# Two Mamba layers on one core: constants cast by ScalarE, projection weights in two tiles loaded in pieces, and a reordered last image

## The chip, the cores and the metric

The kernel runs on one core of one Trainium2 chip. The metric is the device time of one execution in microseconds (us). Three runs are shown for the kernel before, and one further execution was recorded by the hardware profiler.

## The reference, cut to what matters

The input is x, 8 images of 384 channels and 32 x 32 pixels in float32. Four residual layers follow, each on a group norm (32 groups) of x.

```python
x = x + L0(_gn(x))   # Mamba over the 1024 pixels of an image
x = x + L1(_gn(x))   # 1x1 conv, 8x8 FFT filter, depthwise 3x3, gelu(x1)*x2, 1x1 conv
x = x + L2(_gn(x))   # layer norm, Mamba, then gelu(t @ w1.T + b1) @ w2.T + b2
x = x + L3(_gn(x))   # depthwise 3x3 convolution

# Mamba, d_inner 768, 16 states
xin, z = split(xseq @ in_proj_w.T)
u = silu(causal_conv3(xin) + conv_b)
dt, B, C = split(u @ x_proj_w.T);  dt = softplus(dt @ dt_proj_w.T + dt_proj_b)
h = exp(dt*A) * h + (dt*u) * B     # step by step over the pixels
y = (sum_n(h * C) + u*D) * silu(z)
return y @ out_proj_w.T
```

## The kernel before, in words

The pixels of an image make two chunks of T = 512, so each Mamba layer has 16 chunks and both together have 32, numbered n = 0 to 31. Chunks 0 to 15 are layer 0, followed image by image by layer 1 (`layer1`); chunks 16 to 31 are layer 2 with its MLP (`mlp`), followed image by image by layer 3 (`layer3`). A chunk has NQ = 24 scan steps, 768 in all. One step reads 1 MB of dt*u from DRAM into a tile `g` of 128 partitions x 4 x 512 (`begins`, on the SP queue), multiplies it by B on GpSimd (`times`), makes dt by a matmul into the four banks `dA` (`decays`), takes the exponential on ScalarE (`exps`), scans on VectorE (`scans`), multiplies by C half on GpSimd (`states`) and half on VectorE, and sums the states by matmuls into `y` (`gathers`). After four steps a block of 128 channels of y is gated by silu(z) (`gatings`); six blocks make a chunk. Five `g` tiles are in rotation, so the load of step t waits for the sums of step t - 5.

`front(n)` prepares a chunk: norm, the input projection `ps_in` into u, silu, `ps_x`, `ps_dt`, and the DMAs dtd and dud that hand dt and dt*u over through DRAM. `gates(n, h)` makes one half of silu(z) by the projection `ps_z`. `finish(n)` makes the output projection `ps_out` (3 chains of 6 matmuls), and in layer 2 starts `mlp`: per half g, six chains `ps_up` into the tile `h`, an exact gelu over `h` in two instructions, three chains `ps_dn`.

The text writes no order by hand: every one of these pieces is a Python generator, and `Order.run` picks the next instruction by modelled clocks (`Clocks`), due times, `pace` (not before scan step t) and `once` (a condition). What it picks is a fixed order of instructions for each engine and for the SP queue, which issues all DMAs one after the other; at run time each instruction then waits for its own operands, and everything behind it on its queue waits too.

Places that matter below. At the start VectorE casts the constant `selr` (L400) and scales `minus` (L412) before it takes the statistics of the first image (`measure_first`). `load_mamba` (L508) loads all weights of a Mamba layer; it is called from `front` of chunk 0 and of chunk 16. The tile `w_in` has one buffer and holds both halves of the input projection, for u and for z, so layer 2's weights replace layer 0's:

```python
        w["in"] = new(wk, [P, KC, 2 * DI], F32, "w_in")
        for k in range(KC):
            sync.dma_start(w["in"][:, k, :], a[pre + "in_proj"][k * P : (k + 1) * P, :])
```

In `layer3` an image is normed block by block (k = 0, 1, 2) into one padded tile `xp`; each half of a block gets 4 of its 9 taps as matmuls with a diagonal matrix `diag` (made by ScalarE) into `ps_dw`, and the other 5 by VectorE on the PSUM bank. The next block may be normed only when the last has been taken: `yield once(lambda: taken[0] == 2 * k)`.

In the trace nearly all instructions carry L189, the line of the helper that records them, so groups are told apart by their tiles. A float32 matmul shows as two rows of PE.

Of the kernel before, what the change touches and what calls it, by code (L numbers as in the profile page):

```python
# [48 lines left out]
PATIENCE = 6.0  # L49
TAPS, LAST_TAPS = 4, 4  # L50
SHARE = (2, 2, 2, 2)
# [3 lines left out]
def _flat(ap):  # L55
    return ap.rearrange("p a b -> p (a b)")
# [193 lines left out]
def tile_conv_preact_d4(ctx: ExitStack, tc: tile.TileContext, a: dict, out: bass.AP):  # L250
# [148 lines left out]
    sync.dma_start(sel32, a["c_selr"])  # L399
    vector.tensor_copy(_flat(selr), sel32)  # L400
    selbc = const.tile([RX, 2 * P], F32, name="selbc")
# [3 lines left out]
    eps_gn = const.tile([P, 1], F32, name="eps_gn")  # L405
    vector.memset(eps_gn, GN_EPS)
    eps_ln = const.tile([P, 1], F32, name="eps_ln")
    vector.memset(eps_ln, LN_EPS)
    eye = const.tile([P, P], F32, name="eye")
    sync.dma_start(eye, a["c_eye"])  # L410
    minus = const.tile([P, P], BF16, name="minus")
    vector.tensor_scalar_mul(minus, eye, -1.0)  # L412
    carry = const.tile([P, 4 * NQ], F32, name="carry")
# [6 lines left out]
    ln_mean = const.tile([P, P], F32, name="ln_mean")  # L420
    vector.memset(ln_mean, 1.0 / C)

# [4 lines left out]
    xk_free, m_free, x_free = Tokens(1), Tokens(2), Tokens(3)  # L427
    dt_free, pc_free = Tokens(2), Tokens(2)


# [74 lines left out]
    def load_rows(tile_, src, k=KC):  # L505
        sync.dma_start(tile_, src.rearrange("(k p) l -> p k l", k=k))

    def load_mamba(pre):  # L508
        w = {}
        w["vec"] = new(wk, [P, ND, 5], F32, "w_vec", 2)  # L510
        sync.dma_start(w["vec"], a[pre + "vec"])
        w["A"] = new(wk, [P, 4 * NQ], F32, "w_A", 2)
        sync.dma_start(w["A"], a[pre + "A"])
        w["in"] = new(wk, [P, KC, 2 * DI], F32, "w_in")
        for k in range(KC):
            sync.dma_start(w["in"][:, k, :], a[pre + "in_proj"][k * P : (k + 1) * P, :])
        w["x"] = new(wk, [P, ND, RX], F32, "w_x")
        load_rows(w["x"], a[pre + "x_proj"], ND)
        w["dt"] = new(wk, [RX, DI], F32, "w_dt")
        sync.dma_start(w["dt"], a[pre + "dt_proj"])  # L520
        layer_w[pre] = w
        yield on("ACT", w["A"])
        act(w["A"], w["A"], AF.Exp)
        yield on("DVE", w["A"])
        vector.tensor_scalar_mul(w["A"], w["A"], -1.0)

    def load_out(w, pre):
        w["out"] = new(wk, [P, ND, C], F32, "w_out")
        load_rows(w["out"], a[pre + "out_proj"], ND)

    def projection(s, name, at):
        return chain(
            name, ((s["w"]["in"][:, k, at : at + P], s["xn"][:, k, :]) for k in range(KC))
        )
# [13 lines left out]
    def gates(s, h):  # L548
        n = s["n"]
        yield once(lambda: "normed" in s and (n == 0 or chunks[n - 1]["gated"] >= (NH if h == 0 else ND)))  # L550
        z = s["z", h] = new(wk, [P, NH, T], F32, "z", 2)

        def block(d):
            ps, tag = yield from projection(s, "ps_z", DI + (h * NH + d) * P)
# [39 lines left out]
    def front(s):  # L594
# [5 lines left out]
        else:  # L600
            xn = s["xn"] = new(wk, [P, KC, T], F32, "xf", 2)
            sync.dma_start(xn, _rows(s["src"][s["b"], :, c * T : (c + 1) * T]))
        if n % (B * NCH) == 0:
            yield from load_mamba(s["pre"])
        w = s["w"] = layer_w[s["pre"]]
# [13 lines left out]
        def block(d):  # L619
            if n not in (0, B * NCH - 1, B * NCH):  # L620
                yield pace(s["t"] - 18 + d)
            ps, tag = yield from projection(s, "ps_in", d * P)
# [12 lines left out]
        yield from together(due, [block(d) for d in range(ND)])  # L635
        if c > 0:
            yield on("POOL", *u, due=-1)
# [12 lines left out]
        for h in range(2):  # L650
# [3 lines left out]
            "ps_x", ((w["x"][:, d, :], u[d]) for d in range(ND)), place=lambda ps: ps[:RX, :]  # L654
        )
        yield once(lambda: n == 0 or "fronted" in chunks[n - 1])
        yield on("ACT", ps)
# [251 lines left out]
    def finish(s):  # L909
        n, t = s["n"], s["t"]  # L910
        last = s["pre"] == "l2_"
        due = t + NQ + (10 if not last else 23 if s["c"] == 0 else 16)
        yield once(lambda: s["gated"] == ND and (n == 0 or "free" in chunks[n - 1]))

# [9 lines left out]
        else:  # L924
# [5 lines left out]
            s["tt"] = [new(p2, [P, T], F32, "t", KC) for _ in range(KC)]  # L930

        def block(m):
            ps, tag = yield from chain(
                "ps_out",
# [221 lines left out]
    def mlp(s, due):  # L1156
        x = s["x"]

        def weight(q):
            return lambda: None if q >= len(s["loaded"]) else clocks.known(s["loaded"][q])  # L1160

        for g in range(2):
# [4 lines left out]
            def up(f):  # L1167
# [24 lines left out]
            turn = Tokens(1)  # L1192
# [26 lines left out]
    def layer3(s):  # L1219
# [4 lines left out]
        def blocks():  # L1224
            for h in range(2):
                for k in range(KC):
                    yield h, k, x[h][:, k, :], None

        gn = yield from group_stats(blocks)
        taken = [0]  # L1230
        taps = TAPS if b < B - 1 else LAST_TAPS
        for k in range(KC):
            yield once(lambda: taken[0] == 2 * k)
            for h in range(2):
                yield on("ACT", gn[1])
                group_norm(
                    xp[:, 1 + 16 * h : 17 + 16 * h, 1 : W + 1], _img(x[h][:, k, :]), gn
                )
            for hf in range(2):
                yield pace(s["t"] + NQ + 20 + (7 if b < B - 2 else 4) * (2 * k + hf))  # L1240
                rows = slice(hf * 512, (hf + 1) * 512)

                def window(dy, dx, hf=hf):
                    return xp[:, 16 * hf + dy : 16 * hf + dy + 16, dx : dx + W]

                def take(ps, tag, k=k, hf=hf, rows=rows, window=window):
# [6 lines left out]
                    yield on("DVE", ps, when=lambda: 0.0 if taken[0] == 2 * k + hf else None)  # L1253
                    acc = new(p2, [P, T], F32, "acc")
                    vector.tensor_add(acc, ps, x[hf][:, k, :])
# [44 lines left out]
    def diagonal():  # L1300
        yield once(lambda: len(chunks[0].get("dtd", ())) > 0)
        yield on("SP")
# [10 lines left out]

    order.add(measure_first(), 0)
    order.add(front(chunks[0]), 0)
    order.add(begun(), 0)
# [152 lines left out]
```

## Time and profile before

| | us |
|---|---|
| runs: median (lowest to highest of 3) | 6279.72 (6264.88 to 6286.1) |
| profiled execution: own time | 6281.34 |
| profiled execution: span of the trace | 6279.6 |
| busy: PE | 5835.6 (93%) |
| busy: GpSimd (POOL) | 5720.2 (91%) |
| busy: VectorE (DVE) | 5623.6 (90%) |
| busy: ScalarE (ACT) | 4234.9 (67%) |

Times within the trace count from the start of the span. A row of the timeline has the start, the time taken (of all instructions merged into it), the engine, the tiles and the count; the bracket at its end gives the idle time before it on that engine and what ended it. "SPq" rows are issues of DMAs, and a merged row's time runs from its first issue to its last. "PEclk" is the granted clock of TensorE as a share of full speed. Mean granted clock over the execution was 0.965.

### The profile page before, as it was taken

The page shows a single profiled execution, that of the slowest core. Times are in us where ns is not written, and L with a number is a line of the kernel's source. Part 1 is how long each engine was busy: PE and PEld are TensorE (multiplying, and loading weights), DVE is VectorE, ACT ScalarE, POOL GpSimd, SP SyncE. Part 2 cuts the span into 40 slices and gives each one's busy share as a digit, 9 for nine tenths or more (in the row PEclk, how much of TensorE's full clock was granted, in tenths as well). Part 3 has the DMA queues.
Part 4 walks back from the last instruction along what each step waited for, and adds up shares of the span by engine and source line. Part 5 has one row for each costly group of instructions (what it writes and reads, how often), then busy time and mean ns, then how long its engine had stood idle before and what let it go on. Part 6 is the DMA issues. An engine that isn't in the chain of part 4 may idle for free.

```text
span 6279.6 us, 62636 instructions
## 1 busy us (share of the span) xinstructions
PE 5835.6 (93%) x19010; PEld 2196.0 (35%) x19010; DVE 5623.6 (90%) x6392; ACT 4234.9 (67%) x7940; POOL 5720.2 (91%) x2022
## 2 busy tenths in 40 slices
PE   6878999999999999989989999999999999999997
PEld 2223333333333333333333333333333333333333
DVE  4999989999999989988887999999998999989992
ACT  4656677677767667766676766777677676667752
POOL 4999989999998999989997999999999999999980
PEclk8889999999999999999999999999999999999998
DMA  6877878887887878877777888888787787887871
GB/s 174 189 186 185 193 186 194 206 189 192 195 191 182 193 197 199 200 183 179 185 178 182 203 205 208 213 201 209 191 214 195 196 208 189 207 203 197 197 186 35
DMA packets 345860, 1195.88 MB, mean 190 GB/s; under 512 B 40420, under 2 KB 142484, under 8 KB 247220
## 3 DMA queue, kind: packets, MB, share of 16 engines
q1 hardware_dynamic: 345524, 1191.88, 78.0%
q8 instruction: 152, 2.49, 0.2%
q14 instruction: 184, 1.51, 0.1%
HBM read 1040.73 MB, written 150.99 MB: 190 GB/s over the span
## 4 chain that ended last, share of the span: by engine, by line
DVE 18%; PE 14%; POOL 12%; ACT 7%; issue 5%; DMA 3%; SPq 0%; DVEq 0%; POOLq 0%; ACTq 0%
POOL g L189 10%; DVE g L189 8%; DVE dA L189 5%; PE ps_up L189 3%; PE ps_dn L189 2%; PE y L189 2%; DMA g<-dud 2%; DVE ps_dw L189 2%; ACT dA L189 2%; PE dA L189 2%; DVE u L189 1%; PE ps_dw L189 1%; ACT h L189 1%; ACT L370 1%; ACT L189 1%
## 5 line engine op out<-in xcount | busy, mean ns | idle before, releaser
L189 POOL TENSOR_TENSOR g<-g,bc 128x1024 f32<-128x1024 f32 (+1 forms) x1536 | 5241.0, 3445 | 279.4 <-ACT carry L189 111.8
L189 ACT ACTIVATE dA<-dA,w_A 128x512 f32<-128x512 f32 x3072 | 2018.6, 661 | 964.1 <-PE dA L189 952.5
L189 PE MATMUL dA<-dts,selr 96*128 96x512 bf16 x3072 | 1193.7, 391 | 248.1 <-DVE g L189 223.7
L189 DVE TENSOR_TENSOR_SCAN g<-dA,carry,g 128x512 f32<-128x512 f32 x768 | 954.7, 1270 | 70.8 <-POOL g L189 55.2
L189 DVE TENSOR_TENSOR g<-dA,bc 128x512 f32<-128x512 f32 x1536 | 994.5, 678 | 20.4 <-ACT carry L189 18.8
L189 DVE TENSOR_TENSOR_SCAN dA<-dA,carry,g 128x512 f32<-128x512 f32 x768 | 953.8, 1273 | 42.6 <-ACT dA L189 42.1
L189 DVE TENSOR_TENSOR_SCAN dA<-dA,g 128x512 f32<-128x512 f32 x768 | 910.2, 1212 | 65.8 <-ACT dA L189 65.5
L189 DVE TENSOR_TENSOR_SCAN g<-dA,g 128x512 f32<-128x512 f32 x768 | 908.0, 1209 | 61.8 <-POOL g L189 43.9
L189 PE MATMUL y<-g,sely 128*32 128x512 f32 x6144 | 866.9, 632 | 47.0 <-POOL g L189 44.4
L189 PEld LDWEIGHTS <-selr 96*128 96x128 bf16 x3072 | 300.8, 99 | 1117.6 <-issue 1070.2
L189 PE MATMUL ps_in<-xf,w_in 128*128 128x512 f32 x1152 | 574.0, 619 | 3.7 <-ACT xf L189 3.3
L189 PE MATMUL ps_dn<-h,mw 128*128 128x512 f32 x1152 | 556.5, 605 | 13.9 <-ACT h L189 8.0
L189 PE MATMUL ps_z<-xf,w_in 128*128 128x512 f32 x1152 | 564.3, 596 | 4.0 <-DVE dt L189 3.6
L189 PE MATMUL ps_up<-t,mw 128*128 128x512 f32 x1152 | 556.9, 597 | 5.0 <-DVE acc L189 1.8
L189 PE MATMUL ps_out<-u,w_out 128*128 128x512 f32 x1152 | 552.0, 595 | 0.2 <-DVE x L189 0.2
L189 PE MATMUL ps_dw<-tp,diag 128*128 128x512 f32 x864 | 435.0, 606 | 8.9 <-ACT diag L189 8.8
L189 PEld LDWEIGHTS y<-g,sely 128*32 128x32 f32 x6144 | 127.6, 109 | 618.4 <-issue 296.1
L189 PEld LDWEIGHTS ps_dn<-h,mw 128*128 128x128 f32 x1152 | 218.8, 193 | 288.1 <-issue 245.5
L189 PEld LDWEIGHTS ps_in<-xf,w_in 128*128 128x128 f32 x1152 | 220.8, 197 | 273.8 <-issue 237.0
L189 POOL TENSOR_TENSOR dt<-dt,u 128x512 f32<-128x512 f32 x192 | 244.1, 1273 | 74.6 <-ACT pc L189 60.0
L189 PEld LDWEIGHTS ps_up<-t,mw 128*128 128x128 f32 x1152 | 215.6, 191 | 265.6 <-issue 227.5
L189 PEld LDWEIGHTS ps_z<-xf,w_in 128*128 128x128 f32 x1152 | 215.9, 190 | 253.2 <-issue 219.6
(112 smaller groups left out, 6471.2 us busy)
## 6 DMA issues: line engine op xcount, KB each, us to landing
g<-dud SPq DMA_DIRECT2D x768, 1024.0 KB, 7.8
dtd<-pc SPq DMA_DIRECT2D x192, 384.0 KB, 3.9
dts<-dtd SPq DMA_DIRECT2D x192, 384.0 KB, 7.8
mw<-in_l_mlp_w SPq DMA_DIRECT2D x192, 384.0 KB, 6.1
dud<-dt SPq DMA_DIRECT2D x768, 64.0 KB, 3.2
xf<-in_x SPq DMA_DIRECT2D x16, 768.0 KB, 9.2
x<-in_x SPq DMA_DIRECT2D x16, 768.0 KB, 11.4
x_mid<-x SPq DMA_DIRECT2D x16, 768.0 KB, 7.4
```

What stands on the lines that cost most here:

```text
L189: return call(out_, *args, **kw)
L370: nc.scalar.preload_act_table_set(SET_EXP)
```

## The change

- Start: `selr` and `minus` are made by ScalarE (`constants`), and three small fills go from VectorE to GpSimd.
- Weights: `w_in` is split into `w_in` (half for u) and `w_z` (half for z). `load_mamba` is a generator of its own beside `front`; for layer 2 each piece waits, in the planner, until the chunk 15 has made its last use of the old piece and the scan has reached a given step.
- Last chunk (31): `finish` begins when five blocks are gated and the MLP of chunk 30 has ended; its output projection takes blocks as they are gated (`piecewise`). Its MLP applies gelu straight from PSUM, chain by chain, in place of bias and a gelu over the tile.
- Last image in `layer3`: three padded tiles in buffers of `g`, filled with zeros by GpSimd, in place of one; the wait on `taken` is dropped; 5 taps of 9 on TensorE in place of 4; results go to two further buffers of `g`.

```diff
-TAPS, LAST_TAPS = 4, 4
+TAPS, LAST_TAPS = 4, 5
...
-    vector.tensor_copy(_flat(selr), sel32)
...
-    vector.memset(eps_gn, GN_EPS)
+    gpsimd.memset(eps_gn, GN_EPS)
...
-    vector.tensor_scalar_mul(minus, eye, -1.0)
...
+    def constants():
+        yield on("ACT", sel32)
+        act(_flat(selr), sel32, AF.Copy)
+        yield on("ACT", eye)
+        act(minus, eye, AF.Copy, scale=-1.0)
...
-    def load_mamba(pre):
+    def load_mamba(pre, old=None):
+        def free(mark, step):
+            if old is None:
+                yield on("SP")
+            else:
+                yield once(lambda: mark in old)
+                yield pace(old["t"] + step)
+                yield on("SP")
...
+        rows = [a[pre + "in_proj"][k * P : (k + 1) * P, :] for k in range(KC)]
+        yield from free("projected", -11)
         w["vec"] = new(wk, [P, ND, 5], F32, "w_vec", 2)
...
-        w["in"] = new(wk, [P, KC, 2 * DI], F32, "w_in")
+        w["in"] = new(wk, [P, KC, DI], F32, "w_in")
         for k in range(KC):
-            sync.dma_start(w["in"][:, k, :], a[pre + "in_proj"][k * P : (k + 1) * P, :])
+            yield from free("projected", -11 + k)
+            sync.dma_start(w["in"][:, k, :], rows[k][:, :DI])
...
+        yield from free("spread", -8)
         w["x"] = new(wk, [P, ND, RX], F32, "w_x")
...
+        yield from free("fronted", -7)
         w["dt"] = new(wk, [RX, DI], F32, "w_dt")
...
+        yield from free(("gates", 1), 3)
+        w["z"] = new(wk, [P, KC, DI], F32, "w_z")
+        for k in range(KC):
+            yield from free(("gates", 1), 3 + k)
+            sync.dma_start(w["z"][:, k, :], rows[k][:, DI:])
+        w["loaded"] = True
...
-        if n % (B * NCH) == 0:
-            yield from load_mamba(s["pre"])
+        yield once(lambda: s["pre"] in layer_w)
...
+        end = n == len(chunks) - 1
+        if end:
+            yield once(lambda: s["gated"] >= ND - 1 and "ended" in chunks[n - 1])
...
+        def piecewise(m):
+            ps = None
+            for d in range(ND):
+                u = s["u"][d // NH][:, d % NH, :]
+                yield on("PE", u, when=both(
+                    bank if ps is None else lambda: 0.0,
+                    lambda: 0.0 if s["gated"] > d else None,
+                ))
+                if ps is None:
+                    ps, tag = ps_take("ps_out")
+                mm(ps, s["w"]["out"][:, d, m * P : (m + 1) * P], u, d == 0, d == ND - 1)
+            return ps, tag
...
-                act(h1[:, f, :], ps, AF.Identity, bias=b1[:, q : q + 1])
+                act(h1[:, f, :], ps, AF.Gelu if end else AF.Identity, bias=b1[:, q : q + 1])
...
-            yield on("ACT", h1, when=session())
-            for q in range(2):
-                part = _flat(h1[:, 3 * q : 3 * q + 3, :])
-                act(part, part, AF.Gelu)
-            exp_set()
+            if not end:
+                yield on("ACT", h1, when=session())
+                for q in range(2):
+                    part = _flat(h1[:, 3 * q : 3 * q + 3, :])
+                    act(part, part, AF.Gelu)
+                exp_set()
...
+            for k in range(KC):
...
+                wide = new(wk, [P, 4, T], F32, "g", AHEAD + 1)
+                flat = _flat(wide)[:, : (H + 2) * (W + 2)]
+                pads.append(flat.rearrange("p (h w) -> p h w", w=W + 2))
+                gpsimd.memset(flat, 0.0)
+            spare = [new(wk, [P, 4, T], F32, "g", AHEAD + 1) for _ in range(2)]
...
-            yield once(lambda: taken[0] == 2 * k)
+            yield once(lambda: end or taken[0] == 2 * k)
...
+    order.add(constants(), 1)
+    order.add(load_mamba("l0_"), 0)
+    order.add(load_mamba("l2_", chunks[B * NCH - 1]), NQ * B * NCH - 30)
```

`gates` and the load of `w_D` now also wait, in the planner, until the weights are `loaded`.

More of the change, by code (lines that the diff above doesn't have):

```diff
@@ L405, in tile_conv_preact_d4 @@
     eps_gn = const.tile([P, 1], F32, name="eps_gn")
[L406 removed]
+    gpsimd.memset(eps_gn, GN_EPS)
     eps_ln = const.tile([P, 1], F32, name="eps_ln")
[L408 removed]
+    gpsimd.memset(eps_ln, LN_EPS)
     eye = const.tile([P, P], F32, name="eye")
@@ L420, in tile_conv_preact_d4 @@
     ln_mean = const.tile([P, P], F32, name="ln_mean")
-    vector.memset(ln_mean, 1.0 / C)
+    gpsimd.memset(ln_mean, 1.0 / C)
     dAs = [psa.tile([P, T], F32, name=f"dA{j}") for j in range(4)]
@@ L513, in load_mamba @@
         sync.dma_start(w["A"], a[pre + "A"])
-        w["in"] = new(wk, [P, KC, 2 * DI], F32, "w_in")
+        w["in"] = new(wk, [P, KC, DI], F32, "w_in")
         for k in range(KC):
-            sync.dma_start(w["in"][:, k, :], a[pre + "in_proj"][k * P : (k + 1) * P, :])
+            yield from free("projected", -11 + k)
+            sync.dma_start(w["in"][:, k, :], rows[k][:, :DI])
+        if old is None:
+            layer_w[pre] = w
+        yield from free("spread", -8)
         w["x"] = new(wk, [P, ND, RX], F32, "w_x")
         load_rows(w["x"], a[pre + "x_proj"], ND)
+        yield from free("fronted", -7)
         w["dt"] = new(wk, [RX, DI], F32, "w_dt")
@@ L529, in load_out, with projection @@
         load_rows(w["out"], a[pre + "out_proj"], ND)
-    def projection(s, name, at):
+    def projection(s, name, part, at):
         return chain(
-            name, ((s["w"]["in"][:, k, at : at + P], s["xn"][:, k, :]) for k in range(KC))
+            name, ((s["w"][part][:, k, at : at + P], s["xn"][:, k, :]) for k in range(KC))
         )
@@ L549, in gates @@
         n = s["n"]
-        yield once(lambda: "normed" in s and (n == 0 or chunks[n - 1]["gated"] >= (NH if h == 0 else ND)))
+        yield once(lambda: "normed" in s and "loaded" in s["w"] and (n == 0 or chunks[n - 1]["gated"] >= (NH if h == 0 else ND)))
         z = s["z", h] = new(wk, [P, NH, T], F32, "z", 2)
         def block(d):
-            ps, tag = yield from projection(s, "ps_z", DI + (h * NH + d) * P)
+            ps, tag = yield from projection(s, "ps_z", "z", (h * NH + d) * P)
             yield on("ACT", ps)
@@ L621, in block @@
                 yield pace(s["t"] - 18 + d)
-            ps, tag = yield from projection(s, "ps_in", d * P)
+            ps, tag = yield from projection(s, "ps_in", "in", d * P)
             yield on("ACT", ps)
@@ L635, in front @@
         yield from together(due, [block(d) for d in range(ND)])
+        s["projected"] = True
         if c > 0:
@@ L655, in front @@
         )
+        s["spread"] = True
         yield once(lambda: n == 0 or "fronted" in chunks[n - 1])
@@ L912, in finish @@
         due = t + NQ + (10 if not last else 23 if s["c"] == 0 else 16)
-        yield once(lambda: s["gated"] == ND and (n == 0 or "free" in chunks[n - 1]))
+        end = n == len(chunks) - 1
+        if end:
+            yield once(lambda: s["gated"] >= ND - 1 and "ended" in chunks[n - 1])
+        else:
+            yield once(lambda: s["gated"] == ND and (n == 0 or "free" in chunks[n - 1]))
         def load_x():
@@ L930, in finish @@
             s["tt"] = [new(p2, [P, T], F32, "t", KC) for _ in range(KC)]
+        def piecewise(m):
[10 more added lines that the diff above has]
+            return ps, tag
         def block(m):
-            ps, tag = yield from chain(
+            ps, tag = yield from piecewise(m) if end else chain(
                 "ps_out",
@@ L1157, in mlp @@
         x = s["x"]
+        end = s["n"] == len(chunks) - 1
         def weight(q):
@@ L1227, in blocks @@
                     yield h, k, x[h][:, k, :], None
+        end = b == B - 1
+        pads = [xp] * KC
+        if end:
+            yield once(lambda: ahead["scans"] == 4 * len(steps))
+            pads = []
+            for k in range(KC):
+                yield on("POOL", when=lambda: (
+                    0.0 if ("gather", len(steps) - AHEAD + k) in said else None
+                ))
+                wide = new(wk, [P, 4, T], F32, "g", AHEAD + 1)
[3 more added lines that the diff above has]
+            spare = [new(wk, [P, 4, T], F32, "g", AHEAD + 1) for _ in range(2)]
         gn = yield from group_stats(blocks)
         taken = [0]
-        taps = TAPS if b < B - 1 else LAST_TAPS
+        taps = LAST_TAPS if end else TAPS
         for k in range(KC):
-            yield once(lambda: taken[0] == 2 * k)
+            pad = pads[k]
+            yield once(lambda: end or taken[0] == 2 * k)
             for h in range(2):
@@ L1236, in layer3 @@
                 group_norm(
-                    xp[:, 1 + 16 * h : 17 + 16 * h, 1 : W + 1], _img(x[h][:, k, :]), gn
+                    pad[:, 1 + 16 * h : 17 + 16 * h, 1 : W + 1], _img(x[h][:, k, :]), gn
                 )
@@ L1241, in layer3, with window @@
                 rows = slice(hf * 512, (hf + 1) * 512)
-                def window(dy, dx, hf=hf):
-                    return xp[:, 16 * hf + dy : 16 * hf + dy + 16, dx : dx + W]
+                def window(dy, dx, hf=hf, pad=pad):
+                    return pad[:, 16 * hf + dy : 16 * hf + dy + 16, dx : dx + W]
                 def take(ps, tag, k=k, hf=hf, rows=rows, window=window):
@@ L1253, in take @@
                     yield on("DVE", ps, when=lambda: 0.0 if taken[0] == 2 * k + hf else None)
-                    acc = new(p2, [P, T], F32, "acc")
+                    if end:
+                        acc = spare[(2 * k + hf) // 4][:, (2 * k + hf) % 4, :]
+                    else:
+                        acc = new(p2, [P, T], F32, "acc")
                     vector.tensor_add(acc, ps, x[hf][:, k, :])
@@ L1300, in diagonal @@
     def diagonal():
-        yield once(lambda: len(chunks[0].get("dtd", ())) > 0)
+        yield once(lambda: len(chunks[0].get("dtd", ())) > 0 and "loaded" in layer_w["l0_"])
         yield on("SP")
```

## The prediction

> **What bounds the kernel now.** I read the page first, for the engines' shares:
>
> ```profile
> PE 5835.6 (93%) x19010; PEld 2196.0 (35%) x19010; DVE 5623.6 (90%) x6392; ACT 4234.9 (67%) x7940; POOL 5720.2 (91%) x2022
> ```
>
> Three engines are nearly full all the time, so in steady state no single wait bounds it. So I took the places that the change touches one by one. The start, in VectorE's timeline:
>
> ```profile
> 9.83 0.42 DVE L189 CAST selr<-sel 96x512 bf16<-96x512 f32 x1 [9.83 <-DMA sel<-in_c_selr]
> ...
> 10.76 3.60 DVE L189 BATCH_NORM_STATS2 st<-xf 128x6 f32<-128x512 f32 x6
> 14.39 0.32 DVE L189 BATCH_NORM_AGGREGATE mv<-st 128x2 f32<-128x36 f32 x1
> ```
>
> The statistics stand behind the cast, and the cast waits for a DMA. Next the seam between layers 0 and 2: the waits of the SP queue and of GpSimd by total (waited in us, times, longest), and the timelines there:
>
> ```profile
> SPq L189 <- PE ps_z L189: 29.6, 9, 25.3
> ...
> POOL g L189 <- DMA g<-dud: 98.8, 44, 16.8
> ```
>
> ```profile
> 2782.22 0.43 SPq L189 DMA_DIRECT2D w_A<-in_l_A  x1
> 2808.01 1.28 SPq L189 DMA_DIRECT2D w_in<-in_l_in_proj  x3
> ...
> 2810.89 0.53 SPq L189 DMA_DIRECT2D g<-dud  x1
> ...
> 2824.92 4.49 POOL L189 TENSOR_TENSOR g<-g,bc 128x2048 f32<-128x2048 f32 x1 [16.79 <-DMA g<-dud]
> ```
>
> The one 25.3 us wait is `w_in` of layer 2, held until chunk 15's last `ps_z` has read the old tile; the next load of g is behind it on SP, and GpSimd stands for 16.79 us. Then the tail, TensorE's timeline:
>
> ```profile
> 6125.81 5.42 PE L189 MATMUL ps_dn<-h,mw 128*128 128x512 f32 x12
> 6131.06 15.61 PE L189 MATMUL ps_out<-u,w_out 128*128 128x512 f32 x36
> ...
> 6165.70 17.41 PE L189 MATMUL ps_dn<-h,mw 128*128 128x512 f32 x36 [3.57 <-ACT h L189]
> ...
> 6202.14 18.40 PE L189 MATMUL ps_dn<-h,mw 128*128 128x512 f32 x36 [3.57 <-ACT h L189]
> 6230.08 9.50 PE L189 MATMUL ps_dw<-xp,diag 128*128 128x512 f32 x16 [2.76 <-ACT diag L189]
> 6245.71 10.21 PE L189 MATMUL ps_dw<-xp,diag 128*128 128x512 f32 x16 [6.13 <-ACT diag L189]
> ```
>
> After the last sum into y (ends 6125.9) TensorE alone sets the end: no scans are left. 36 warm rows take 15.61 us (0.43 each). Last, layer 2's steady state by windows of about two chunks (its fastest and slowest: PE busy and rows, then the others):
>
> ```profile
> 3410.00:3788.00 378.00, 369.19 (x1188) 140.33 (x1187) 342.01 (x387) 265.14 (x464) 361.19 (x133) 1.00 0.84 205
> 4550.00:4950.00 400.00, 382.13 (x1227) 143.68 (x1226) 367.38 (x418) 277.86 (x490) 372.12 (x140) 0.98 0.81 201
> ```
>
> TensorE is busy for 97% of either: layer 2 is TensorE's.
>
> **The change part by part.** Beside the profile I have the order of instructions that the planner writes for the changed kernel, a list without times.
>
> *Start.* The casts leave VectorE. The completion events of the second load of x lie at 7.7 to 8.6 us, so three statistics (1.8 us) run before it and three after: the last ends at about 10.5 instead of 14.36. Gain 3.9. The casts on ScalarE (96x512 to bf16: nearest row, pc<-dt 128x512, 0.61, against 0.42 on VectorE) begin at 9.8 and 10.5 and end by 11.0, before `ps_gn` asks ScalarE (now 15.39, then 11.5); were it busy, they would cost 0.9. The fills go to an idle GpSimd. The first `ps_in` at 16.2 instead of 20.13 needs `w_in`; it now lands by half the bytes, so by about 15 where the whole landed by 18.1 (issue at 10.4, 7.7 to landing). `w_z` adds three issues of 0.43 to SP, 40 us before SP is needed.
>
> *Seam.* In the new order `w_in` comes at g loads 354 to 356, `w_x` at 357, `w_dt` at 362, all after the last reader (ps_in of chunk 15 ends 14 steps ahead of it), and `w_z` at 365 to 367, behind `ps_z`, which ends in step 361. So SP no longer stands for 25.3 us. What is late next: the load for step 365 behind the first `w_z`. It needs the sums of step 360 anyhow, about when `ps_z` ends, so at most a step is lost from a lead of five. The same queue held layer 2's first xf and an x load, so front(16) starts some 25 us earlier (its norm was at 2814.6). Bounds: 16.8, plus up to 18 more from the long steps that followed (13.7, 15.6 and 15.5 us in chunks 15 and 16 against 8), down to 0, since TensorE did 10 us of work in the stall which now needs another place. I take 15: TensorE was only 90% busy from 2796 to 3197, so there is room.
>
> *Layer 2.* No instruction changes there, but the planner's order does: before, fronts of odd chunks slip (first `ps_dt` 5 or 6 steps ahead of the chunk in 25 to 31); after, each pair repeats one pattern (8 ahead). Work is the same, so TensorE's rate bounds it: 8465 rows from 3410 to 6126 (2716 us, chunks 18 to 31), 0.321 a row; at the fastest window's 0.318 the rows take 2694. That is 22; the other bound is a loss of 20 if the pattern meets waits that the planner's clocks don't know. I take 12, near the fast windows' rate, which had similar placement.
>
> *Tail before the last y.* The last `ps_dn` of chunk 30 (5.2 us) and five of the 18 matmuls of `ps_out` (10 rows, 4.3) now stand before the last y. Sum 9.5; TensorE idles 16 us in 5733 to 6126, some 8 of them in the last chunk, so not all may fit: 6 (bounds 0 and 9.5). The other 13 matmuls start with ten that need no new gating (8.6 us), which covers y's gating (1.5). Only the last three wait for it, with `ps_up` queued behind; uncovered it would cost 1.7.
>
> *MLP of chunk 31.* Gelu from PSUM takes the place of bias (0.69) plus gelu (2.85 per tile). The last h is ready 0.9 us after `ps_up`, while `ps_dn` needs it as the sixth operand, 4.3 us in. Both gaps of 3.57 go, and with them the slow rows after them (17.41 and 18.40 against 15.61): 7.1 + 4.6 = 11.7. The gelu table's load (1.28) falls into the 2.6 us of the first `ps_up` chain.
>
> *Last image.* Before, 6230.08 to 6276.5 (last add): 46.5. After, 30 taps run without a stop: first chain 10 rows 4.3 + 2.6 for the cold start (16 rows took 9.50 against 6.9) + 0.2 = 7.1; five more chains 21.7; then 4 taps and an add by VectorE, 3.8: 32.6. VectorE needs 3.8 per chain (under 4.3), ScalarE 5.5 per block (under 8.7). GpSimd's fills (3, about 1 us each by tp's 2.98 for three times the size) hide in the MLP. The table for exp, preloaded before in the MLP's shade, now stands between `gsp` and `grstd`: +0.6, as at the start (16.23 + 1.28, while `ps_gn` was there at 16.85). Gain 13.3.
>
> Two rules of the Trainium skill bear on this. Row: 1283 ns for every table load. "ScalarE: Activation LUTs", Rules for kernel authors, budgets about 2.7 us for every switch to another set: then the exposed load would cost 2.0 instead of 0.6, and the gelu load would come out level with the first chain; the row decides. Row: 9.50 us for 16 rows after a pause. "TensorE: Matmul & The Clock Gate", What's actually happening: after an idle window of about 3.4 us the clock is half until 3.4 us of work are done. By that rule a cold start costs 1.7, not 2.6, the first chain 6.2 and the gain 14.2. I keep the row.
>
> Sum: 3.9 + 15 + 12 + 6 + 11.7 + 13.3 = 62. The profiled execution's own time, 6281.3 (span 6279.6 and 1.7 around), becomes 6219; it lies 1.6 above the median of the runs, so against the median 6218.
>
> **The rivals.** (1) *Layer 2 gains more* (chance 0.2): if all pairs run in 377.5 like the first two (18 to 21), the four of 385, 400, 394 and 389 give 58 in place of 12: 6172. For it, the regular order; against it, the fast pairs did only 1188 rows, and a steady pair has 1208. (2) *TensorE takes it back* (0.15): work from the stall is done later, so the seam and layer 2 give nothing; start and tail remain, 35: 6245. For it: the 43 us step at 3356 to 3399, in which TensorE is never idle for 2 us; the new order has the same lump there. (3) *Slower* (0.06): the new order of layer 2 makes every pair like the slowest, 400 against a mean of 388: 7 x 12 = 84 lost, 50 gained elsewhere: 6314. Place: chunks 18 to 31, where one late `ps_dt` stalls the next chunk's first step. It decides from a mean pair of 395. Against it: windows with this placement were the fast ones. (4) *It does not do what it says*: the listed order shows the pieces, the gelus and the 30 taps in place; 0.04 for a smaller gain near zero, with SP waiting on a piece somewhere.
>
> **How the numbers follow.** Likeliest, 0.55: 6218, with the bounds of its terms 6195 to 6240. The range reaches down to rival 1 and up past rival 2: 6172 to 6250. About 0.3% (19 us) is what a measurement can tell from no change; the forecast and rivals 1 and 2 lie beyond it: faster 0.91, same 0.04, slower 0.05.
>
> **What would show it.** Start: statistics from about 6.5 us, first `ps_in` near 16.2. Seam: no `ps_z` wait of SP over 8 us, no GpSimd wait on g<-dud of 16 us. Tail: `ps_dn` rows at 15.6 without the 3.57; one run of `ps_dw` rows; last y to end near 120 us where it was 154. Layer 2: pairs of 377 to 392. Wrong if the pairs pass 395, or if SP stands behind a weight piece.

## The result, and the profile after

| | before | after |
|---|---|---|
| median of 4 runs, us (lowest to highest) | 6275.32 (6264.88 to 6286.1) | 6203.06 (6198.06 to 6209.78) |
| profiled execution: own time, us | 6281.34 | 6204.07 |
| mean granted clock of TensorE | 0.965 | 0.973 |

The ratio is 0.9886 (95% interval 0.9872 to 0.9901): the kernel became 72 us faster (62 to 80). The forecast was 6218, 15 us too high: the gain was 10 larger than forecast, and the median of the kernel before, now of four runs, is 4 lower than the 6280 from which the forecast was counted. The engines' shares on the page of the kernel after:

```profile
PE 5799.2 (94%) x19022; PEld 2184.1 (35%) x19022; DVE 5616.8 (91%) x6381; ACT 4241.3 (68%) x7942; POOL 5725.3 (92%) x2028
```

TensorE has 12 rows more (the fifth tap) and is busy 36 us less, so the same work ran at a better rate and with fewer pauses. Below, rows are called warm where TensorE's granted clock is full (36 rows in 15.61 us), and cold where it is lower after a pause. The start, first VectorE's timeline, then TensorE's:

```profile
6.09 1.88 DVE L189 BATCH_NORM_STATS2 st<-xf 128x6 f32<-128x512 f32 x3 [6.09 <-DMA xf<-in_x]
10.11 1.88 DVE L189 BATCH_NORM_STATS2 st<-xf 128x6 f32<-128x512 f32 x3 [2.15 <-DMA xf<-in_x]
```

```profile
17.73 8.54 PE L189 MATMUL ps_in<-xf,w_in 128*128 128x512 f32 x13 [3.25 <-ACT xf L189]
```

The statistics no longer stand behind the cast, but their second half waits for the second load of x until 10.11. The first `ps_in` comes at 17.73, where it came at 20.13. The seam, by the waits of the SP queue and of GpSimd (waited in us, times, longest):

```profile
SPq L189 <- PE ps_z L189: 16.9, 9, 12.5
```

```profile
POOL g L189 <- DMA g<-dud: 76.8, 45, 6.3
```

SP's longest wait on `ps_z` went from 25.3 to 12.5, not away: it now stands ahead of `w_z`. GpSimd's longest wait on a load of g went from 16.8 to 6.3. The tail, TensorE's timeline:

```profile
6078.07 4.56 PE L189 MATMUL ps_out<-u,w_out 128*128 128x512 f32 x10
6082.56 1.25 PE L189 MATMUL y<-g,sely 128*32 128x512 f32 x8
6083.74 11.43 PE L189 MATMUL ps_out<-u,w_out 128*128 128x512 f32 x26
...
6110.45 15.61 PE L189 MATMUL ps_dn<-h,mw 128*128 128x512 f32 x36
...
6167.28 27.64 PE L189 MATMUL ps_dw<-g,diag 128*128 128x512 f32 x60 [3.53 <-ACT diag L189]
```

From the end of the last y to the end of the span it took 153.7 us and now takes 118.4. Both runs of `ps_dn` take 15.61 without a gap ahead of them (the second starts at 6141.35), and the taps are one run.

Last, layer 2 in its two stretches, chunks 18 to 29 and chunks 30 and 31 (a window's bounds and length, PE busy and rows, then the other engines, granted clock, DMA share, GB/s). First the kernel before, then the kernel after:

```profile
3399.50:5722.60 2323.10, 2250.99 (x7230) 852.75 (x7229) 2152.50 (x2445) 1628.50 (x2884) 2207.28 (x818) 0.99 0.83 203
5722.60:6101.30 378.70, 365.18 (x1180) 137.24 (x1179) 356.35 (x406) 251.21 (x450) 358.10 (x131) 0.99 0.82 200
```

```profile
3376.90:5693.40 2316.50, 2255.51 (x7276) 854.04 (x7275) 2162.88 (x2459) 1646.84 (x2902) 2216.03 (x822) 1.00 0.83 205
5693.40:6060.70 367.30, 352.02 (x1136) 132.40 (x1135) 343.78 (x391) 245.75 (x437) 350.06 (x127) 0.99 0.83 203
```

The kernel after does 46 rows more in the twelve chunks in less time, and so has 44 fewer left for the last two.

To compare many kernels, the span is cut below at GpSimd's first multiplication of a chunk (chunks 0, 14, 18, 30) and at that of the very last scan step. "From the last step" runs to the end of the span. Each column is one execution; all are in us. Kernels whose written order is the same in a stretch show the scatter.

| kernel | start of chunk 0 | chunks 0-13 | 14-17 | 18-29 | 30-31 | from the last step |
|---|---|---|---|---|---|---|
| before | 72.3 | 2519.5 | 807.7 | 2323.1 | 378.7 | 178.3 |
| after | 69.9 | 2510.1 | 796.9 | 2316.5 | 367.3 | 141.5 |
| start alone (e1) | 71.2 | 2519.0 | 806.4 | 2324.1 | 377.7 | 178.3 |
| weights alone (e2) | 71.5 | 2518.4 | 797.5 | 2312.5 | 367.2 | 172.6 |
| tail alone (e3) | 73.9 | 2516.0 | 801.0 | 2325.0 | 377.3 | 153.1 |
| start and weights (e4) | 69.3 | 2518.6 | 794.8 | 2313.3 | 367.2 | 172.0 |
| after, no piecewise (f1) | 71.3 | 2517.3 | 796.9 | 2313.2 | 366.8 | 146.1 |
| after, old gelu (f2) | 69.2 | 2520.2 | 796.6 | 2313.1 | 366.5 | 155.6 |
| after, old image (f3) | 70.4 | 2520.7 | 799.6 | 2313.0 | 366.9 | 155.9 |
| after, 4 taps (f4) | 69.1 | 2517.5 | 800.5 | 2314.6 | 367.1 | 139.8 |
| pieces together (g1) | 68.6 | 2512.4 | 791.3 | 2329.5 | 379.8 | 153.1 |
| w_z later (g2) | 68.1 | 2518.2 | 797.5 | 2313.5 | 366.6 | 142.5 |
| fronts later (g3) | 69.0 | 2518.9 | 797.0 | 2344.7 | 380.7 | 154.0 |
| early statistics (h1) | 70.4 | 2509.6 | 794.6 | 2314.4 | 367.2 | 137.3 |

### The profile page after: what moved, and what is told of

It reads as the page before. It is cut to its first block, busy times and chain, and to the rows that moved or that the text cites. A ratio compares the mean times of both kernels' runs of the same rounds, so it can differ in the third digit from the quotient of the medians.

```text
span 6202.2 us, 62614 instructions
## 1 busy us (share of the span) xinstructions
PE 5799.2 (94%) x19022; PEld 2184.1 (35%) x19022; DVE 5616.8 (91%) x6381; ACT 4241.3 (68%) x7942; POOL 5725.3 (92%) x2028
## 4 chain that ended last, share of the span: by engine, by line
DVE 25%; PE 13%; POOL 8%; DMA 4%; issue 4%; ACT 4%; SPq 0%; POOLq 0%; DVEq 0%; ACTq 0%
DVE g L189 11%; DVE dA L189 8%; POOL g L189 6%; DVE u L189 2%; PE ps_dn L189 2%; PE ps_up L189 2%; PE ps_dw L189 2%; PE y L189 2%; PE dA L189 2%; DMA g<-dud 2%; DVE ps_dw L189 1%; PE ps_z L189 1%; DMA dts<-dtd 1%; PE ps_out L189 1%; DVE st L189 1%
## 5 line engine op out<-in xcount | busy, mean ns | idle before, releaser
L189 PE MATMUL ps_z<-xf,w_z 128*128 128x512 f32 x1152 | 567.8, 597 | 3.6 <-DVE dt L189 3.6
L189 PEld LDWEIGHTS ps_z<-xf,w_z 128*128 128x128 f32 x1152 | 215.9, 191 | 252.7 <-issue 215.2
```

Of the source, the lines that this page charges most:

```text
L189: return call(out_, *args, **kw)
```

## The experiments

My theory: the parts that the prediction named bring the gain at their own places, the stretches of this table. Its rivals: the planner's new order of layer 2 brings it, whatever the weights do; or the parts interact, so that none is worth alone what it is worth with the others.

### The three parts one by one

**Start alone (e1).**

```diff
-    vector.tensor_copy(_flat(selr), sel32)
-    vector.tensor_scalar_mul(minus, eye, -1.0)
+    order.add(constants(), 1)      # both by ScalarE; three fills to GpSimd
```

> The kernel before with the start part alone (casts by ScalarE, fills by GpSimd). The written order of TensorE and of the SP queue stays that of before from the first instruction to the last, and those of the other engines differ only in the moved casts and fills. Theory A (the start gains what its own path shows and no more): step 0 begins about 2.4 us earlier and nothing else changes, so 2 to 4 us, ratio 0.9993 to 0.9997. Rival B (the start carries all that layer 0 gained in the kernel after): 11.8 us by the start of chunk 14, ratio 0.998. Rival C (the start is made up for by the next wait): within 1 us of zero.

Measured: 6272.01, ratio 0.9997 (0.9989 to 1.0005), which excludes B and, by time alone, can't tell A from C. The trace can: first `ps_in` is at 17.43, where it was at 20.13. In this one execution chunk 0 begins only 1.1 us earlier, but over all executions it begins at 69.7 on average with this part (11 of them, 68.1 to 71.3) and at 72.6 without it (3, 71.5 to 73.9). That is 2.9 us, with chunks 0 to 13 as before: theory A. The other 9.4 us by which chunks 0 to 13 were shorter in the profile of after are no effect of the change. In that stretch kernels with the same written order (after, f2, f3, g2, h1) took 2509.6 to 2520.7 us, and the mean of the three kernels with the old weights is 2518.2, that of the other eleven 2516.5.

**Weights alone (e2).**

```diff
-        if n % (B * NCH) == 0:
-            yield from load_mamba(s["pre"])
+    order.add(load_mamba("l2_", chunks[B * NCH - 1]), NQ * B * NCH - 30)
...                                # and w_in split into w_in and w_z
```

> The kernel before with the weights part alone (w_in and w_z, loaded in pieces by a process of its own); the start and the last image stay as before. From the first step of the last chunk backwards its written order is that of the kernel after. Theory A: it carries the seam (10.8 us in chunks 14 to 17) and the shift of 18 us in chunks 18 to 31, and of layer 0 nothing, so 29 us, ratio 0.9954. Rival B (the new order costs in layer 2 what the seam gains, and the 18 us come from elsewhere): 0 to 12 us. Rival C: it also carries the 9 us of layer 0 that the start can't explain, because w_in lands in halves and later fronts move: 38 us, ratio 0.994.

Measured: 6239.64, ratio 0.9945 (0.9932 to 0.9959), 35 us, the largest of the three. Seam 797.5 against 807.7, chunks 18 to 31 in 2679.7 against 2701.8 (22 us, also within 30 and 31: 11.5), and 5.7 in the last stretch, where `ps_dn` of chunk 30 now ends ahead of the last y. Chunks 0 to 13 gave 1.1, so rival C falls; A had missed the 5.7.

**Tail alone (e3)**: the edits of `finish`, `mlp` and `layer3` from the diff of the change, on the kernel before.

> The kernel before with the tail part alone: out-projection by gated block, gelu from PSUM in the last chunk, last image unchained with 5 taps on TensorE. The written order up to the last chunk's out-projection is that of before, and because the MLP of chunk 30 still ends behind the last sum into y, the out-projection by block changes no place on TensorE. Theory A (the blockwise part is worth nothing without the earlier end of chunk 30): gelu 11.7 and image 13.3 as in the prediction, 25 us, ratio 0.996. Rival B (the tail is worth 36.8 us wherever the rest is): ratio 0.9941. As its first 31 chunks have the order of before, their lengths against the first profile show how much they differ from execution to execution: theory A says under 2 us in each chunk.

Measured: 6247.28, ratio 0.9960 (0.9947 to 0.9972). From the last step 153.1 against 178.3: 25.2, where A said 25. The 18 matmuls of `ps_out` still stand behind the last y: without the weights' order the piecewise part has no place to go to. Its seam, in before's order, took 801.0 where before took 807.7: so much do two executions differ there, more than the 2 us that A allowed.

**Start and weights (e4)**: the kernel after without those three edits.

> The kernel after without its tail part: start and weights. Theory A (the parts add up): the sum of start alone and weights alone, about 2.4 + 29 = 31 to 41 us, ratio 0.9935 to 0.995, so that the tail's own share in the kernel after is 31 to 41 us. Rival B (start and weights interact, the layer 0 gain of 11.8 appears only with both): their sum falls short of this kernel by 8 us or more.

Measured: 6233.41, ratio 0.9939 (0.9926 to 0.9951), 38 us by the ratio, near the sum of the two (2 + 35): theory A. The parts add up but for one: the tail brings 172.0 - 141.5 = 30.5 on top of these, 25.2 on its own.

### The tail's pieces, each undone in the kernel after

**Out-projection whole again (f1).**

```diff
-        if end:
-            yield once(lambda: s["gated"] >= ND - 1 and "ended" in chunks[n - 1])
+        yield once(lambda: s["gated"] == ND and (n == 0 or "free" in chunks[n - 1]))
...
-            ps, tag = yield from piecewise(m) if end else chain(
+            ps, tag = yield from chain(
```

> The kernel after with the last chunk's out-projection taken whole, when all six blocks are gated. Only TensorE's order changes, by one move: five of the 18 matmuls of ps_out go from between the last two groups of y to behind them. Theory A (TensorE alone sets the end there, as the prediction put it): the ten rows, 4.3 us, come back behind the last y, and the wait for y's gating is open again, 1 to 2.5 us: 5 to 7 us more from the last sum into y to the end, ratio to before 0.9896. Rival B (the matmuls fill a wait on VectorE's last scan either way, or the cold clock eats them): under 2 us.

Measured: 6214.91, ratio 0.9910 (0.9895 to 0.9925); from the last step 146.1 against 141.5, 4.6 us. Its TensorE timeline shows why the ten rows cost nothing in the kernel after:

```profile
6085.61 2.88 PE L189 MATMUL y<-g,sely 128*32 128x512 f32 x8 [3.56 <-POOL g L189]
6088.42 15.72 PE L189 MATMUL ps_out<-u,w_out 128*128 128x512 f32 x36
```

Without them TensorE stands for 3.56 us ahead of the last y, which waits for GpSimd, and the y after the pause is cold and takes 2.88 in place of 1.25. Theory A had the size nearly (4.6 for 5 to 7), B the place: the rows fill a wait.

**Gelu as before (f2).**

```diff
-                act(h1[:, f, :], ps, AF.Gelu if end else AF.Identity, bias=b1[:, q : q + 1])
+                act(h1[:, f, :], ps, AF.Identity, bias=b1[:, q : q + 1])
...
-            if not end:
```

Gelu then runs over the tile, followed by the load of the exp table, in every chunk.

> The kernel after with the last chunk's gelu as before: bias from PSUM, then gelu over the tile in two instructions. Only ScalarE's order changes. Theory A: two gaps of 3.57 us come back in TensorE's rows, and the slow rows after each: 17.4 and 18.4 us for 36 rows where 15.61 is the warm time, 11.7 us together less 0.6 for the exp table load which is hidden again: 11 us, ratio to before 0.9904. Rival B (a pause of 3.57 us costs only itself): 7.1 us less 0.6.

Measured: 6219.98, ratio 0.9916 (0.9902 to 0.9929); from the last step 155.6 against 141.5, 14.1 us. Its TensorE timeline:

```profile
6119.77 18.58 PE L189 MATMUL ps_dn<-h,mw 128*128 128x512 f32 x36 [3.57 <-ACT h L189]
...
6157.37 18.55 PE L189 MATMUL ps_dn<-h,mw 128*128 128x512 f32 x36 [3.57 <-ACT h L189]
```

Two gaps of 3.57 and two slow runs, 2.97 and 2.94 over the warm 15.61: 13.1 us. So a pause costs what it lasts and some more, against rival B. That "some more" isn't fixed, and the granted clock over the same rows gives its size (all after a pause of 3.57 us; in us):

| run | 36 rows took | over the warm 15.61 | granted clock over the rows | time x (1 - clock) |
|---|---|---|---|---|
| e4 | 17.26 and 17.41 | 1.65 and 1.80 | 0.91 and 0.90 | 1.6 and 1.7 |
| before | 17.41 and 18.40 | 1.80 and 2.79 | 0.90 and 0.85 | 1.7 and 2.8 |
| f2 | 18.58 and 18.55 | 2.97 and 2.94 | 0.84 and 0.85 | 3.0 and 2.8 |

In each case the trace's clock stood at half for one stretch, of which 3.1 to 3.4 us fell on the rows in the first three runs and 5.4 to 5.8 in the others. Why it was longer in one execution than in another isn't shown.

**Last image as before (f3)**: the hunks of `layer3` undone, `LAST_TAPS = 4`.

> The kernel after with the last image as before: one padded tile, blocks chained by the count of finished halves, 4 taps on TensorE. Theory A: the 13.3 us of the prediction come back between the first tap and the last add (46 us against 31.5 in the kernel after: 14.5), ratio to before 0.9909. Rival B (the chain was bound by VectorE's taps and not by the waits of a block on the block before it): 5 taps of 9 on VectorE, 4.6 us a half, 6 halves, 28 us and the first chain's 6: about 3 us.

Measured: 6220.97, ratio 0.9919 (0.9907 to 0.9932); from the last step 155.9 against 141.5, 14.4 us: theory A. The pauses of 6.14 between blocks are back in TensorE's timeline, and each run of taps after one is cold:

```profile
6176.46 10.19 PE L189 MATMUL ps_dw<-xp,diag 128*128 128x512 f32 x16 [3.39 <-ACT diag L189]
6192.78 8.86 PE L189 MATMUL ps_dw<-xp,diag 128*128 128x512 f32 x16 [6.14 <-ACT diag L189]
6207.78 9.89 PE L189 MATMUL ps_dw<-xp,diag 128*128 128x512 f32 x16 [6.14 <-ACT diag L189]
```

**Four taps, still unchained (f4).**

```diff
-TAPS, LAST_TAPS = 4, 5
+TAPS, LAST_TAPS = 4, 4
```

> The kernel after with 4 taps on TensorE in place of 5 in the last image, still unchained with three padded tiles. Theory A (with 5 taps TensorE and VectorE are level, with 4 VectorE is the bound): a half takes VectorE 5 taps of 0.79 and an add of 0.69 and a wait of 0.4, 5.0 us in place of 4.3 on TensorE: six halves give 4 us, less 0.9 for the shorter first chain: 3 us over the kernel after, so that of the 14.4 us which the last image brought some 11 are the dropped wait between blocks and 3 the fifth tap. Rival B (the fifth tap is most of it): 8 us or more.

Measured: 6210.40, ratio 0.9898 (0.9885 to 0.9912); from the last step 139.8, which is 1.7 *less* than in the kernel after. Both theories fall. TensorE's and VectorE's timelines:

```profile
6175.21 19.09 PE L189 MATMUL ps_dw<-g,diag 128*128 128x512 f32 x40 [3.54 <-ACT diag L189]
6194.65 3.67 PE L189 MATMUL ps_dw<-g,diag 128*128 128x512 f32 x8 [0.35 <-DVE g L189]
```

```profile
6180.43 4.65 DVE L189 SCALAR_TENSOR_TENSOR ps_dw<-g,vec,ps_dw 128x512 f32<-128x512 f32 x6 [10.91 <-PE ps_dw L189]
...
6204.56 0.69 DVE L189 TENSOR_TENSOR g<-ps_dw,x 128x512 f32<-128x512 f32 x1
```

VectorE is the bound as A said, but 30 taps and 6 adds run without a stop from 6180.43 to 6205.25, 0.69 us each on average, where I had taken 0.79 and a wait of 0.4 per half. Without the wait for TensorE between halves VectorE is quicker than 30 taps on TensorE (27.64 us). From the first tap to the last add it took 30.0 us with four taps and 31.5 with five, one execution of each. So all of the last image's gain comes from the unchained blocks; the fifth tap brings nothing and seems to cost a little.

### Seam and layer 2

**All pieces together behind the last `ps_z` (g1).**

```diff
-        yield from free("projected", -11)
+        yield from free(("gates", 1), 3)
...                                # no other wait for any piece
```

> The kernel after with the weights still in two tiles but all pieces of layer 2 issued together at the place of the first piece of w_z, behind the last ps_z of chunk 15. So SP stands again with five loads of w_in, w_x, w_dt and w_vec behind that wait, and the front of chunk 16 comes later. In the written order, layer 2 loses its repeating pattern too: first ps_dt of the chunks 19 to 31 stand 5 to 10 steps ahead of the chunk, 8 to 10 in the kernel after. Theory A (the seam gained by the early pieces, layer 2 by its regular, earlier fronts): chunks 14 to 17 lose about 10 us and chunks 18 to 31 about 18 to 22, sum 30, ratio to before 0.9935. Rival B (the stall at the seam is all there is, layer 2's shift comes from anything): chunks 14 to 17 lose 10, the rest stays within 5. Rival C (the split itself brings it, not the place of the pieces): under 5 in all.

Measured: 6236.39, ratio 0.9945 (0.9932 to 0.9957). The size is as A had it, the places are not. The planner put the pieces two loads of g later than before, when `ps_z` was done, so SP's queue did not stand, as its waits show:

```profile
SPq L189 <- PE ps_z L189: 5.0, 9, 0.8
```

The seam became shorter, 791.3, but TensorE also did 21 rows fewer in it than in the kernel after (2424 against 2445), some 7 us by an estimate at its 0.33 us a row, so for the same work it is neither better nor worse. All that is lost is in layer 2 (2709.3 for chunks 18 to 31, against 2683.8) and in the last stretch (11.6). So early pieces are not what the seam needs, and layer 2 hangs on its order.

**`w_z` later (g2).**

```diff
-        yield from free(("gates", 1), 3)
+        yield from free(("gates", 1), 6)
...
-            yield from free(("gates", 1), 3 + k)
+            yield from free(("gates", 1), 6 + k)
```

> The kernel after with the three pieces of w_z paced three steps later. The written orders of TensorE, VectorE, ScalarE and GpSimd are those of after, instruction by instruction; only eight places in the SP queue differ, so that SP no longer stands 12.5 us before the first piece of w_z. Theory A (what the seam is worth is the time that SP stands there): chunks 14 to 17 take 791 to 793 us instead of 796.9, as in the run with all pieces together, where SP stood for less than 1 us and they took 791.3; 4 to 6 us gained, ratio to before 0.9878. Rival B (the 12.5 us are covered by the five loads of g ahead; the seam is TensorE's): within 2 us of the kernel after.

Measured: 6203.31, ratio 0.9890 (0.9876 to 0.9903), the time of after; seam 797.5. SP's wait was removed:

```profile
SPq L189 <- PE ps_z L189: 4.1, 7, 0.6
```

Removing 12.5 us of standing on SP brought nothing: rival B. The loads ahead of it covered it: in the kernel after GpSimd waited for no load of g longer than 0.95 us from 2735 to 2840, the time around the 12.5.

**Fronts one step later (g3).**

```diff
-                yield pace(s["t"] - 18 + d)
+                yield pace(s["t"] - (17 if n > 18 else 18) + d)
```

> The kernel after with one number changed: from chunk 19 on the input projections are paced one scan step later (17 steps ahead in place of 18). Weights, start and the last image are as in after; up to chunk 18 the written order is the same. From there layer 2 loses its repeating pattern: first ps_dt 3 to 10 steps ahead of its chunk in place of 8 and 10 in turn, and the MLP of a chunk ends 51 to 58 steps after the chunk's begin in place of 51. Theory A (layer 2's gain of about 20 us is the repeating pattern, and no property of the weights): chunks 18 to 31 take 2701 to 2710 us as in the kernel before and in the run with all pieces together, in place of 2680 to 2684, and as the MLP of chunk 30 ends later the out-projection by block finds no place, 5 to 6 more: 25 us in all, ratio to before 0.9925. Rival B (it is the early weights and fronts at the seam that bring it): within 5 us of the kernel after.

Measured: 6265.37, ratio 0.9984 (0.9977 to 0.9990): one number takes 62 of the 72 us away, two and a half times what A expected. Windows of chunks 18 to 29, 30 and 31, and from the last step:

```profile
3384.80:5729.50 2344.70, 2254.32 (x7216) 852.75 (x7215) 2151.57 (x2442) 1634.80 (x2885) 2207.40 (x817) 0.99 0.82 201
5729.50:6110.20 380.70, 363.79 (x1178) 136.14 (x1177) 356.45 (x406) 250.71 (x450) 358.38 (x130) 0.99 0.82 199
6110.20:6264.20 154.00, 135.63 (x334) 57.70 (x332) 54.23 (x70) 43.33 (x76) 14.60 (x8) 0.95 0.16 49
```

Against the kernel after it did 60 rows fewer in chunks 18 to 29 with 28 us more, paid for those rows in the last two chunks and the last stretch, and lost the place of the piecewise out-projection. TensorE's own longest class of waits in the first of these stretches, before, after and here:

```profile
PE dA L189 <- DVE g L189: 36.5, 72, 4.9
```

```profile
PE dA L189 <- DVE g L189: 28.8, 76, 1.4
```

```profile
PE dA L189 <- DVE g L189: 52.7, 103, 3.5
```

In these waits the matmul that makes the next steps' dt waits until VectorE is done with the bank `dA`. They are only a part. By the windows above TensorE stood still for 72.1 us in chunks 18 to 29 before, 61.0 after and 90.4 here (length less busy time), and a row took it 311.3, 310.0 and 312.4 ns (busy time by rows), at a granted clock of 0.99, 1.00 and 0.99. So for the same rows the kernel before paid 11 us more in pauses than after and 10 in slower rows, and this one 29 and 17. The slower rows go with the clock: in this stretch it stood at half for 27 us before, at no time after, and for 44 us here.

Weights and seam were those of after, so rival B falls: layer 2's gain lies in its written order. That the regular pattern is what counts in it is argued. It fits the four orders that were run (chunks 18 to 31: the regular one 2680 to 2684 us; the others 2702 in before, 2709 in g1, 2725 here), but here the fronts were also one step later, and the result is worse than before.

**Early statistics (h1)**: g2 and two edits.

```diff
-            yield on("DVE", v)
+            yield on("DVE", v, when=when(h, k) if when else None)  # block final
...
+            elif g == 1:           # last MLP, behind its last gelu
+                yield on("ACT")
+                exp_set()
```

> The kernel with w_z three steps later, and two edits behind the last MLP: the statistics of the last image are taken block by block as its blocks become final (five of six before the last one's add, 0.61 us each), and the exp table is loaded behind the last gelu and not between the two group sums. Theory A: 5 x 0.61 = 3.0 and 0.6 us off the path from the last add of the MLP to the first tap, 3.6 together: from the start of the last step to the end 137.9 us against 141.5, on top of what the later w_z brings; ratio to before 0.987 to 0.9885. Rival B (the longer pause's end only moves, and TensorE starts the taps cold either way with slower rows): 1 to 2 us.

Measured: 6198.32, ratio 0.9884 (0.9869 to 0.9900). From the last step 137.3 (expected 137.9), against 141.5 and, in g2, 142.5: theory A. TensorE's pause ahead of `ps_gn` is 1.86 where it was 4.70; first the kernel after, then this one:

```profile
6161.66 0.59 PE L189 MATMUL ps_gn<-mv,gmat 128*128 128x1 f32 x2 [4.70 <-DVE mv L189]
```

```profile
6153.83 0.38 PE L189 MATMUL ps_gn<-mv,gmat 128*128 128x1 f32 x2 [1.86 <-DVE mv L189]
```

It is the best version that was run, but 4 to 5 us in its last stretch are too few for its time to be told from that of after. By an estimate from f4, four taps would make it some 1.5 shorter still; that was not run.

## Why the prediction was right, and where its terms were wrong

The forecast of a clear gain held and its sum was 62; the runs show 72 (62 to 80). By terms, with the differences of the table as the measure:

| term | predicted | measured | from |
|---|---|---|---|
| start | 3.9 | 2.9 | chunk 0's start, means of 3 and 11 |
| seam | 15 | 7.8 | chunks 14-17: 805.0 in before's order (3 executions), 797.2 in after's (10) |
| layer 2 | 12 | 21 | chunks 18-31: 2702.0 (3), 2680.8 (9) |
| before the last y | 6 | 11 | 6.3 (before to e4) and 4.6 (f1) |
| MLP of chunk 31 | 11.7 | 11 to 14 | pauses and slow rows in before, e4, f2 |
| last image | 13.3 | 14.4 | f3 |

They sum to 68 to 71. That the sum came close is in part luck, as errors of both signs offset each other: seam 7 too high, layer 2 and the last y 14 too low.

**Start.** The failed step is "the completion events of the second load of x lie at 7.7 to 8.6 us". In seven of the eleven executions with this part VectorE was released for it only at 9.53 to 10.14, first `ps_in` came at 17.2 to 17.8 (16.2 forecast), and chunk 0 began at 70.2 on average. In the other four (f2, g1, g2, g3) VectorE was released at 8.10 to 8.22, `ps_in` came at 15.7 to 15.9, and chunk 0 began at 68.7, which is the 3.9 of the forecast before 72.6. So the term holds where the load lands in time, and most often it did not; what sets that is not shown.

**Seam.** The failed step is "I take 15": 7.8 was measured. It put the gain at SP's stall and GpSimd's wait of 16.8, that is in chunk 15, and left out that the new order also puts more work into these chunks. Chunk 15 took 203.1 us for 593 rows before and 195.1 for 572 after, 0.34 us a row in both. The long steps that made the upper bound (against 8 they add 21, not 18) did not go: the kernel after still has steps of 17.1, 13.7 and 14.7 us in this chunk and one of 16.0 in the next. The gain lies in chunk 16, first before, then after:

```profile
2987.70:3185.60 197.90, 177.69 (x603) 71.24 (x603) 171.91 (x200) 131.47 (x300) 181.71 (x70) 0.91 0.76 185
2974.10:3159.50 185.40, 169.71 (x604) 68.04 (x604) 172.03 (x202) 129.43 (x291) 174.81 (x64) 0.97 0.78 187
```

The rows (603 and 604) took 12.5 us less: 8.0 of busy time, at a higher granted clock, and 4.5 of pauses. Chunks 14 and 17 did 22 and 12 rows more and became 6.2 and 3.5 longer. Over the four chunks TensorE did 15 rows more (2430 to 2445), some 5 us by an estimate at 0.33 us a row, so on equal rows the seam gained about 13, near the 15; the last stretch has these rows fewer. Whether chunk 16 gained by the stall that is gone or by its new order is not shown. The forecast "no `ps_z` wait over 8 us" failed too (12.5), and with it the prediction's own sign of being wrong, that SP stands behind a weight piece; g2 shows that it was worth nothing. The stall of 25.3 outlasted five tiles of g; the one of 12.5 did not.

**Layer 2.** The mechanism stood: TensorE bounds it, and in its new order it comes near its fastest rate, about half by fewer pauses and half by faster rows (under g3). It was busy for 98% and 96% of the two windows that the prediction shows, not for 97% of either. The mis-sized term is "I take 12": 21 is nearly the bound of 22 that came from the fastest window's rate, of which I took half. It did not come as the fast pairs promised (rival 1). Pairs took 385 to 387 where I had said 377 to 392, and half of the gain, 10.9 on average, came in the last pair, because rows had been done earlier. Rival 3 did not happen, but g3 shows that it was nearer than 0.06: with a pace moved by one step, six pairs of 378.7 to 419.4, 391 on average (not yet 395), and what they cost in the tail leave a gain of 0.16%. The edits of the change do not ensure a good order of layer 2; the prediction had the listed order and did not ask how easily it is lost.

**Before the last y.** The ten moved rows were counted as 4.3 at most; as they fill a wait of 3.56 and spare the cold y behind it, they are worth 4.6, and none of the moved rows delayed the last y: from the start of the last step to its end it took 24.6 us before and 23.1 after.

**MLP and last image.** Working and rows as predicted (`ps_dn` at 15.61, `ps_dw` in one run). Two details failed. The fifth tap is not needed for balance (f4). And "I keep the row" took the dearer cold start: 2.6 us by the row, where the half clock of the Trainium skill ("TensorE: Matmul & The Clock Gate", What's actually happening) gave an estimate of 1.7. In the kernel after the 60 rows took 27.64, 1.6 over their warm 26.0, and these 1.0 less are most of what the term of 13.3 lacked of 14.4. Yet neither price is fixed: in the eight executions with these 60 rows in one run they took 27.5 to 29.0, so 1.5 to 3.0 over, at granted clocks of 0.94 to 0.89; the same section says that the number of slow matmuls varies from run to run. The row of 1283 ns for a table load held: the next activation began 1.29 us after the load's start, 0.6 us were exposed, and h1 took them away together with the statistics.

## What to carry to other kernels

Where a planner writes the order, an edit can re-plan everything behind it (g1, g3) or nothing (g2), and that is a term of its own, here as large as the largest intended one. Test it by an edit that should do nothing (a pace moved by one step), and price it by how many rows TensorE has done by a fixed chunk. Compare stretches on equal rows: a stretch can look better because it did less. A queue's stall costs only what outlasts the loads ahead of it. At the end of a kernel, where one engine runs alone, each pause costs itself and the slow rows after it, and the granted clock over these rows gives their price.

## What the runs showed of the hardware that I had not expected

- The same pause costs differently: 36 matmul rows after 3.57 us without work took between 17.26 and 18.58 us, in one case 17.41 and 18.40 within one execution. In every case the excess is about the time multiplied by the missing share of the granted clock (0.91 to 0.84 over the rows).
- VectorE's taps on a PSUM bank lasted 0.75 us each in the kernel after and in f4 alike, overlapping. In f4's unbroken run the next tap of a half began 0.66 to 0.86 us after the last, in after's groups of four 0.79 to 0.86. What sets this distance stays open.
- Executions with one written order differ by up to 11 us in chunks 0 to 13 and by 6 to 7 in chunks 14 to 17, but only by 4 in chunks 18 to 31; three of the fourteen executions (after, g1, h1) had chunk 3 in 175.2 us, the others in 176.4 to 177.3. These three are also the ones with the shortest chunks 0 to 13 (2509.6 to 2512.4), where TensorE was busy for 2292 to 2294 us and in the others for 2297 to 2305, with the same work. What sets this stays open.
